# A graph-attention layer on one NeuronCore: edge rows loaded after all of x, layer-norm subtractions on other engines, the first products in two token groups, two weight splits and two output sums later in the order

## The chip, the cores and the metric

The kernel runs on one NeuronCore of a Trainium2 chip. The time is the device time of one execution in microseconds (us); the table gives the median of three runs. A core has five engines that run side by side, each with its own queue of instructions in program order: PE (matrix products), DVE (vector), ACT (scalar activations), POOL (GpSimd) and SP, which here only issues DMA transfers. An instruction that needs a result of another engine, or of a transfer, waits at the head of its queue, and everything behind it in that queue waits with it.

## The reference

N = 384 tokens, 1024 features, 16 heads of 64; a graph of 6528 edges.

```python
h = jnp.maximum(_layernorm(x, axis=-1), 0.0)
q = h @ wq.T + bq;  k = h @ wk.T + bk;  v = h @ wv.T + bv
q2 = (q @ wiq.T + biq).reshape(N, H, D).transpose(1, 0, 2)      # the same for k2, v2
mask = _build_mask(edge_index, edge_type, edge_type_weights, x.dtype)   # -inf where no edge
scores = jnp.einsum('hnd,hmd->hnm', q2, k2) * scale + mask[None]
out = jnp.einsum('hnm,hmd->hnd', softmax(scores), v2)
return x + out.transpose(1, 0, 2).reshape(N, OUT_F) @ wo.T + bo
```

## The kernel before, in words

**Precision.** Every operand of a product is held as two parts in a reduced format, `hi` and `lo` = value - hi. A product of a weight and an activation is three matmuls (`mm3`, L367 to L369): hi by hi, hi by lo, lo by hi.

**Weights.** Seven weight matrices come in 56 chunks of 128 x 1024 (512 KB), numbered w: 0-7 are wv, 8-15 wq, 16-23 wiv, 24-31 wk, 32-47 wiq and wik in turn, 48-55 wo. A chunk goes through `load` (SP issues a DMA into one of three `raw` buffers), `split_hi` (ACT, L77, a cast) and `split_lo` (L82, a subtraction, on DVE or on POOL), into one of four `whl` buffers.

**The head.** SP issues the loads of the three 128-token tiles of x (L96), with the edge rows `er` (L98, 128 x 102 integers) between tile 0 and tile 1, then weight 0, the edge table `ed`, weight 1, biases. PE turns dummy transposes over (`warm`, L309). `key_rows` (L180: three POOL operations L182 to L184 and a store) makes the edge keys row by row in `krow`, from which `key_load` (L205) reads them back into all partitions. For each tile t the layer norm takes mean and variance on DVE (`ln_bn`, `ln_mean`), subtracts the mean in two halves of 512 (`ln_sub`; on ACT by a bias `negm`, on POOL L282, or on DVE L284), transposes on PE (`ln_transpose`, L292) and keeps max(0, .) as hi (ACT, `ln_hi`, L298) and lo (DVE, `ln_lo`, L303). The division by the standard deviation comes later, as a row (`ln_row`). POOL makes both parts of weight 0 (L344, L346) and the low part of weight 1 (L82).

**Projections.** `proj` runs slots: one chunk of 128 outputs by all 384 tokens, 24 matmuls in one PSUM bank. Slot 0 (L411) does its 24 in an order by what is ready: hi-hi for k = 0..7, then lo-hi and hi-lo by halves of k. Meanwhile the edge mask is made: DVE compares keys, POOL scatters values into DRAM.

**The attention loop.** `for i in range(S + LA + 4)` (L767) works step i on 48 pairs of a head and a token tile: score product S(i) (L694, PSUM tag `s`, two banks), mask, minimum and read-out on DVE for i-1 (L700), exponential for i-2 (ACT, L704), normalisation for i-3 (POOL, L709), transposes for i-5 (L714), their split for i-6 (`do_pt`, L723 on ACT, L724 on DVE), products with v (L731). Between them `fill` draws other PE work from generators: first `fill_qk` (the q and k products of chunks 32 to 47), then `fill_o` (the output products `omm`).

At the beginning of a chunk of `fill_qk` a task `qk_head(w)` is queued, which runs at the end of that step (before the loop at once): it loads chunk w+4, splits w+2, and takes one `qk_done` from `pendq`: evacuation of the last bank (L377, L378) and the copies of its halves into `qs` (L557 to L560) or `ks` (L567), DMAs from SBUF to SBUF. `PRE = 84` puts chunks 32, 33, 34 and half of 35 ahead of step 0. With `PAR = 1` odd chunks have their low half on POOL.

In the second half, `wo_prep(k)` splits chunk 48+k at the steps `WSTEPS`; `OPOOL` lists the k with the low half on POOL. After the fourth product of an output bank, `ysum` (L654, DVE) adds the bank to x + bo.

Of the kernel before, what the change touches and what calls it, by code (L numbers as in the profile page):

```python
# [14 lines left out]
N, D, NT, KT, NP = 384, 1024, 3, 8, 8  # L15
# [7 lines left out]
def gnn_kernel(ctx: ExitStack, tc: tile.TileContext, x, edges, erows, etw, wq, wk, wv, wiq, wik, wiv, wo,  # L23
# [6 lines left out]
    nc = tc.nc  # L30
# [9 lines left out]
    NTAB, RNG = 3, EC // 3  # L40
# [3 lines left out]
    def bank(tag):  # L44
        return psum.tile([128, 512], F32, tag=tag, name=tag, bufs={"g": 3, "a": 1}.get(tag, 2))
# [14 lines left out]
    def load(w):  # L60
        if w >= NCH:
            return
        n, m = chunks[w]
        raw[w] = wpool.tile([128, D], F32, tag="raw", name="raw", bufs=3)
        nc.sync.dma_start(raw[w], W[n][m])
# [28 lines left out]
    er = ert[:, :2 * EC].bitcast(I32)  # L94
    for t in range(NT):
        nc.sync.dma_start(xt[t], x[t * 128:(t + 1) * 128, :])  # L96
        if t == 0:
            nc.sync.dma_start(er, erows)  # L98
    load(0)
    ed = const.tile([128, 3 * EC], I32, name="ed")  # L100
    nc.sync.dma_start(ed, edges)
# [78 lines left out]
    def key_rows():  # L180

        nc.gpsimd.tensor_copy(kf, er)  # L182
        nc.gpsimd.tensor_scalar(kf[:, :EC], kf[:, :EC], float(N), None, op0=OP.mult)
        nc.gpsimd.tensor_tensor(krt[:, :EC], kf[:, :EC], kf[:, EC:], OP.add)  # L184
        nc.sync.dma_start(krow.rearrange("c j -> (c j)").rearrange("(p e) -> p e", p=128), krt[:, :EC])
# [10 lines left out]
    def key_load(g, s):  # L196

        if s == 0:
            t = work.tile([128, 2, NT, N], F32R, tag="pt", name="rows")
            krv[g] = t.bitcast(F32).rearrange("p a k n -> p (a k n)")  # L200
        c0, c1 = parts(g)[s]
        dst = krv[g][:, s * PA * 128:(s * PA + c1 - c0) * 128]
        for c in range(c0, c1):
            rows[c] = krv[g][:, (s * PA + c - c0) * 128:(s * PA + c - c0 + 1) * 128]
        nc.sync.dma_start(dst, krow[c0:c1, :].rearrange("c j -> (c j)").partition_broadcast(128))  # L205
# [44 lines left out]
    def ln_bn(t, h):  # L250
        nc.vector.bn_stats(lnt[:, 30 + 12 * t + 6 * h:36 + 12 * t + 6 * h], xt[t][:, h * 512:(h + 1) * 512])

    def ln_mean(t):
        nc.vector.bn_aggr(lnt[:, 2 * t:2 * t + 2],
                          lnt[:, 30 + 12 * t:42 + 12 * t].rearrange("p (a b) -> p a b", a=2))
        if t < 2:
            nc.scalar.mul(negm[:, t:t + 1], lnt[:, 2 * t:2 * t + 1], -1.0)

    def ln_root():
# [17 lines left out]
    def ln_sub(t, c0, c1, eng):  # L277
        src, dst = xt[t][:, c0:c1], xn[t][:, c0:c1]
        if eng is nc.scalar:
            nc.scalar.activation(dst, src, AF.Identity, bias=negm[:, t:t + 1])  # L280
        elif eng is nc.gpsimd:
            nc.gpsimd.tensor_tensor(dst, src, lnt[:, 2 * t:2 * t + 1].to_broadcast([128, c1 - c0]), OP.subtract)  # L282
        else:
            nc.vector.tensor_scalar(dst, src, lnt[:, 2 * t:2 * t + 1], None, op0=OP.subtract)  # L284

    def ln_transpose(t):
        pss = []
        for half in range(2):
            ps = bank("st"[half] if t < 2 else "ga"[half])
            for j in range(4):  # L290
                k = half * 4 + j
                nc.tensor.transpose(ps[:, j * 128:(j + 1) * 128], xn[t][:, k * 128:(k + 1) * 128], ident)  # L292
            pss.append(ps)
        return pss

    def ln_hi(t, half, ps):
        hi = hT[:, 0, half * 4:half * 4 + 4, t * 128:(t + 1) * 128]
        nc.scalar.activation(hi, ps.rearrange("p (k n) -> p k n", k=4), AF.Relu)  # L298
# [7 lines left out]
    def warm(n):  # L306
        for i in range(n):
            ps = bank("g")
            nc.tensor.transpose(ps[:, :128], ident, ident)  # L309

    mask_consts()
    warm(WARM[0])
    key_rows()
    load(2)
    for s in range(NTAB):
        key_load(0, s)
    ln_bn(0, 0)
    ln_bn(0, 1)
    ln_mean(0)
# [6 lines left out]
    ln_bn(1, 0)  # L326
    ln_bn(1, 1)
    ln_mean(1)
    ln_sub(1, 0, 512, nc.scalar)
    ln_sub(1, 512, D, nc.gpsimd)  # L330
    ln_bn(2, 0)
    ln_bn(2, 1)
    ln_mean(2)
    ln_sub(2, 0, 512, nc.vector)
    ln_sub(2, 512, D, nc.vector)
    p1 = ln_transpose(1)
    warm(WARM[2])
    ln_hi(1, 0, p1[0])
    ln_hi(1, 1, p1[1])
    p2 = ln_transpose(2)  # L340
    t0 = wpool.tile([128, 2, D], F32R, tag="whl", name="whl", bufs=4)
    whl[0] = (t0[:, 0, :], t0[:, 1, :])
# [43 lines left out]
    w = 0  # L386
# [18 lines left out]
    def proj(src, dst, bidx, extra=None):  # L405
        nonlocal w
        for m in range(8):
            slot_head(w)
            ps = bank("g")
            if w == 0:  # L410
                for a, b, ks in ((0, 0, range(KT)), (1, 0, range(4)), (0, 1, range(4)), (1, 0, range(4, KT)),  # L411
                                 (0, 1, range(4, KT))):
                    for k in ks:
                        nc.tensor.matmul(ps[:, :N], whl[0][a][:, k * 128:(k + 1) * 128], src[:, b, k, :],  # L414
                                         start=(a == b == k == 0), stop=(b == 1 and k == KT - 1))
            else:
                for k in range(KT):
                    colmm(ps, w, src, k)
                    if w == 1 and k == 3:
                        ln_row()  # L420
                        flush()
            pend.append(lambda ps=ps, m=m: evac_row(ps, dst[:, 0, m, :], dst[:, 1, m, :],
                                                bc[:, bidx * 8 + m:bidx * 8 + m + 1]))
            if extra:
                extra(m)
            w += 1
# [145 lines left out]
    def run_tasks():  # L572
        while tasks:
            tasks.pop(0)()

    def qk_head(w):
        first = w - W0 < 3
        if not first:
            load(w + 4)
            split_hi(w + 2)  # L580
        if pendq:
            pendq.pop(0)()
        if 0 < w - W0 < NTAB:
            mask_select(w - W0)
        if first:
            split_hi(w + 2)
        split_lo(w + 2, nc.gpsimd if (w + 2) % 2 == PAR else None)
        if first:
            load(w + 4)
        if w == W0:  # L590
            mask_select(0)
# [21 lines left out]
    LT, LA = 5, 7  # L613
    PRE, RATE, RATE_O, RATE_E = 84, 7.9, 8, 8
    WSTEPS = (37, 40, 42, 44, 47, 51)
    PAR, OPOOL, ODVE = 1, (2, 3, 6), (2,)

    otile = {}
    oacc = {}
# [31 lines left out]
    def ysum(a, c=(0, 512)):  # L651
        t, h = OT[a]
        y = xb[t][:, h * 512 + c[0]:h * 512 + c[1]]
        nc.vector.tensor_tensor(y, oacc[t, h][:, c[0]:c[1]], y, OP.add)  # L654
        return y

    def fill_o():


        first = [(0, 0), (0, 1), (1, 0), (1, 1), (2, 0), (2, 1)]  # L660
        first += [(a, k) for k in (2, 3) for a in range(3)] + [(a, k) for a in range(3, 6) for k in range(KH)]
        for a, k in first:
            while now[0] < wready[k] or now[0] < 6 * k + OREADY or (k == KH - 1 and now[0] < XSTEP + 3):
                yield 0
            if k == 0:
                oacc[OT[a]] = bank("g")
            omm(*OT[a], k)
            if k == KH - 1:
                ysum(a)
            yield 4  # L670
        bank_step = (0, 0, 0, 49, 50)
        todo = [(a, k) for k in range(KH, 7) for a in range(5)]
        while todo:
            ready = [q for q in todo if now[0] >= max(6 * q[1] + OREADY, wready[q[1]], bank_step[q[0]])]
            if not ready:
                yield 0
                continue
            a, k = ready[0]
            todo.remove(ready[0])
            if k == KH:  # L680
                oacc[OT[a]] = bank("gggss"[a])
            omm(*OT[a], k)
            yield 4
# [83 lines left out]
    for i in range(S + LA + 4):  # L767
        now[0] = i
        r = RATE if len(gens) == 2 else RATE_O if i < S else RATE_E
        fill(r / 2)  # L770
        if i < S:
            do_S(i)
        fill(r / 2)
        if 0 <= i - 1 < S:
            do_ttr(i - 1)
        if 0 <= i - 2 < S:
            do_exp(i - 2)
        if 0 <= i - 3 < S:
            do_norm(i - 3)
        if 0 <= i - LT < S:  # L780
            do_T(i - LT)
        j = i - LA
        if j >= 2 and (j - 2) % 3 == 0 and (j - 2) // 3 < 16:
            do_A((j - 2) // 3)
        if 0 <= i - LT - 1 < S:
            do_pt(i - LT - 1)
        if j >= 3 and (j - 3) % 3 == 0 and (j - 3) // 3 < 16:
            do_ao((j - 3) // 3)
        if j >= 4 and (j - 4) % 6 == 3:
            do_aos((j - 4) // 3)  # L790
        run_tasks()
        if i == XSTEP:
            assert len(gens) < 2
            xb_load()
        if i in WSTEPS:
            wo_prep(wp)
            wready[wp] = i + 2
            wp += 1
# [57 lines left out]
```

## Time and profile before

| | us |
|---|---|
| median of 3 runs | 303.16 (302.75 to 303.68) |
| the profiled execution | 302.19 |
| its span, first to last instruction | 300.5 |
| first product with a weight (L414) starts | 12.26 |
| last matmul ends, modelled | 296.98 |

The granted PE clock is 0.999 of full speed. What PE waited for, by the profile (instruction, releaser: us in total, times, longest):

```profile
PE s L292 <- ACT g L280: 2.0, 2, 1.2
PE g L309 <- POOL ident masks.py:199: 1.4, 1, 1.4
PE s L694 <- DVE s L700: 0.2, 1, 0.2
```

In a timeline a row has the start in us, the length in us, engine, line, operation, output<-input, shapes, the count merged in that row, and in brackets the idle time of the engine before it with what ended it. In the rows of windows each engine has its busy time in the window, and behind them stand the granted PE clock, the busy share of the 16 DMA engines and GB/s. A line number is that of the kernel before.

### The profile page before, as it was taken

To read this page: it belongs to the slowest core of one execution; us is meant where nothing else is said; L and a number is where in the kernel's file an instruction comes from. 1 tells how busy PE (TensorE), PEld (TensorE's weight loads), DVE (VectorE), ACT (ScalarE), POOL (GpSimd) and SP (SyncE) were. 2 spreads that over 40 slices of the span, in tenths; PEclk is the share of its full clock that TensorE was granted. 3 is DMA by queue.
4 is the path that set the end of the run, shared out by engine and by line. 5 is a ranking of instruction groups with operands and counts; after the bars stand their busy time and mean duration, and the time that the engine had idled before them with its cause. 6 is when DMAs were issued, how large, how long until landed. Compare 5 with 4: busy or idle time off the path is not lost.

```text
span 300.5 us, 4961 instructions
## 1 busy us (share of the span) xinstructions
PE 293.1 (98%) x1649; PEld 276.1 (92%) x1649; DVE 200.5 (67%) x492; ACT 154.9 (52%) x289; POOL 155.7 (52%) x164
## 2 busy tenths in 40 slices
PE   7899999999999999999999999999999999999995
PEld 5699999999988889999999999999999998888884
DVE  2959986655956463788865576767576757696523
ACT  3874644333422213554325667777777767676310
POOL 5865766271555785730033737373746467566210
PEclk9999999999999999999999999999999999999999
DMA  7899754642686668475369997646565636910005
GB/s 233 284 297 381 281 164 171 228 143 70 217 238 224 193 217 242 142 274 198 115 169 244 217 221 173 166 127 180 155 170 139 174 81 174 381 41 0 2 0 209
DMA packets 22377, 55.12 MB, mean 183 GB/s; under 512 B 4816, under 2 KB 8400, under 8 KB 22352
## 3 DMA queue, kind: packets, MB, share of 16 engines
q1 hardware_dynamic: 19968, 52.42, 57.7%
q0 software_dynamic: 2064, 1.80, 2.0%
q10 hardware_dynamic: 320, 0.59, 0.8%
q8 instruction: 13, 0.21, 0.3%
q14 instruction: 12, 0.10, 0.1%
HBM read 40.39 MB, written 4.97 MB: 151 GB/s over the span
## 4 chain that ended last, share of the span: by engine, by line
PE 95%; DMA 2%; DVE 1%; ACT 0%; issue 0%; SPq 0%
PE g L369 21%; PE g L367 21%; PE g L368 21%; PE s L694 6%; PE a L731 6%; PE t L714 5%; PE s L369 2%; PE s L368 2%; PE s L367 2%; DMA g<-in_x_dram 2%; PE t L369 2%; PE t L367 2%; PE t L368 2%; PE g L414 1%; PE a L369 1%; PE a L367 1%
## 5 line engine op out<-in xcount | busy, mean ns | idle before, releaser
L367 PE MATMUL g<-g,whl 128*128 128x384 f32 x312 | 106.4, 341 | 0.0
L369 PE MATMUL g<-g,whl 128*128 128x384 f32 x312 | 104.5, 335 | 0.0
L368 PE MATMUL g<-g,whl 128*128 128x384 f32 x312 | 104.2, 334 | 0.0
L228 POOL DMA_INDIRECT tab<-val,idx x51 | 57.6, 1129 | 40.3 <-issue 11.3
L77 ACT ACTIVATE whl<-raw 128x1024 fp32r<-128x1024 f32 x51 | 53.4, 1051 | 31.7 <-PE g L369 20.1
L709 POOL TENSOR_TENSOR e<-e,s 128x384 f32<-128x384 f32 x48 | 39.2, 830 | 41.2 <-DVE s L708 32.9
L368 PEld LDWEIGHTS g<-g,whl 128*128 128x128 f32 x312 | 58.7, 188 | 0.0
L367 PEld LDWEIGHTS g<-g,whl 128*128 128x128 f32 x312 | 58.6, 188 | 0.0
L369 PEld LDWEIGHTS g<-g,whl 128*128 128x128 f32 x312 | 58.5, 188 | 0.0
L82 DVE TENSOR_TENSOR whl<-raw,whl 128x1024 fp32r<-128x1024 f32 x41 | 50.2, 1224 | 9.6 <-ACT whl L77 7.9
L82 POOL TENSOR_TENSOR whl<-raw,whl 128x1024 fp32r<-128x1024 f32 x11 | 26.5, 2412 | 35.6 <-ACT whl L77 31.8
L383 ACT ACTIVATE g<-f,bc 128x384 fp32r<-128x384 f32 x24 | 14.8, 618 | 53.1 <-DVE f L382 46.8
L704 ACT ACTIVATE e<-e,s 128x384 f32<-128x384 f32 x48 | 29.4, 612 | 13.0 <-DVE s L700 13.0
L724 DVE TENSOR_TENSOR pt<-t,pt 128x384 fp32r<-128x384 f32 x48 | 26.4, 550 | 13.9 <-ACT pt L723 13.3
L723 ACT ACTIVATE pt<-t 128x384 fp32r<-128x384 f32 x48 | 23.2, 484 | 13.9 <-PE t L714 13.3
L700 DVE CUSTOM_DVE_ANT_0 e<-s,ma 128x384 f32<-128x384 f32 x48 | 26.3, 550 | 2.0 <-PE s L694 1.8
L694 PE MATMUL s<-ks,qs 128*128 128x384 f32 x96 | 25.3, 344 | 0.3 <-DVE s L700 0.2
L714 PE MATMUL t<-ident,e 128*128 128x128 f32 x144 | 23.5, 271 | 0.0
L382 DVE TENSOR_TENSOR f<-g,rrow 128x384 f32<-128x384 f32 x24 | 13.3, 555 | 13.5 <-PE g L369 7.6
L714 PEld LDWEIGHTS t<-ident,e 128*128 128x128 f32 x144 | 18.8, 140 | 3.1
L378 DVE SCALAR_TENSOR_TENSOR nat<-g,bc,nat 128x384 fp32r<-128x384 f32 x16 | 9.9, 618 | 16.4 <-ACT nat L377 14.4
L731 PE MATMUL a<-pt,vhl 128*128 128x384 f32 x96 | 20.8, 351 | 0.0
(147 smaller groups left out, 414.8 us busy)
## 6 DMA issues: line engine op xcount, KB each, us to landing
ks<-nat SPq DMA_DIRECT2D x30, 192.0 KB
raw<-in_wv_dram SPq DMA_DIRECT2D x8, 512.0 KB
raw<-in_wq_dram SPq DMA_DIRECT2D x8, 512.0 KB
raw<-in_wiv_dram SPq DMA_DIRECT2D x8, 512.0 KB
raw<-in_wk_dram SPq DMA_DIRECT2D x8, 512.0 KB
raw<-in_wiq_dram SPq DMA_DIRECT2D x8, 512.0 KB
raw<-in_wik_dram SPq DMA_DIRECT2D x8, 512.0 KB
raw<-in_wo_dram SPq DMA_DIRECT2D x8, 512.0 KB
```

The source lines that it names most:

```text
L77: nc.scalar.activation(dst[0], raw[w], AF.Copy)
L82: (eng or nc.vector).tensor_tensor(lo, raw[w], hi.bitcast(F32), OP.subtract)
L228: nc.gpsimd.indirect_dma_start(out=tabs[c // RNG], out_offset=bass.IndirectOffsetOnAxis(ap=idx[:, c:c + 1], axis=0), in_=val[:, c:c + 1], ...
L367: nc.tensor.matmul(ps, lhi, rhi, start=first, stop=False)
L368: nc.tensor.matmul(ps, lhi, rlo, start=False, stop=False)
L369: nc.tensor.matmul(ps, llo, rhi, start=False, stop=last)
L694: nc.tensor.matmul(ps[:, :N], qs[:, o, t * 128:(t + 1) * 128], ks[:, o, s, :], start=(s == 0), stop=(s == 1))
L704: nc.scalar.activation(es[i], es[i], AF.Exp, bias=s[:, 0:1], scale=-1.0, accum_out=s[:, 1:2])
L709: nc.gpsimd.tensor_tensor(es[i], es[i], s[:, 2:3].to_broadcast([128, N]), OP.mult)
L714: nc.tensor.transpose(ps[:, k * 128:(k + 1) * 128], es[i][:, k * 128:(k + 1) * 128], ident)
L724: nc.vector.tensor_tensor(lo, pv, hi.bitcast(F32), OP.subtract)
L731: nc.tensor.matmul(ps[:, :N], vhl[:, k, p, 2 * o:2 * o + 2, :], pts[h][:, s, k, :], start=(k == 0 and s == 0), stop=(k == 2 and s == 1))
```

## The change

1. The load of `er` is issued after the three tiles of x.
2. Tile 1's first half is subtracted on DVE in place of ACT, tile 2's second half on ACT in place of DVE; `negm` is made for tiles 0 and 2. In DVE's queue tile 1's subtraction now stands before tile 2's statistics.
3. `key_rows`, `load(2)` and the three `key_load` are emitted after the subtractions of tile 1, and so `key_rows` follows both subtractions in POOL's queue.
4. Tile 1's transposes and hi parts are emitted before tile 2's statistics.
5. Slot 0 does hi-hi for tokens 0 to 255 and then for 256 to 383: 32 matmuls in place of 24.
6. `qk_head` of chunks 35 and 36 only takes its `qk_done` and puts the split of chunks 37 and 38, and the loads of 39 and 40 behind each, off to the ends of steps 2 and 3 (`qk_split`).
7. `ysum` after the fourth product is put in a list, which is emptied after the step's L700 (or when a bank is opened). Two sums of step 43 move behind the L700 of that step; the others keep their place.
8. Chunk 52 (k = 4 of wo) has its low half on POOL.

The order of all other instructions on each engine stays as it was.

```diff
@@ loads
     for t in range(NT):
         nc.sync.dma_start(xt[t], x[t * 128:(t + 1) * 128, :])
-        if t == 0:
-            nc.sync.dma_start(er, erows)
+    nc.sync.dma_start(er, erows)
@@ ln_mean
-        if t < 2:
+        if t != 1:
             nc.scalar.mul(negm[:, t:t + 1], lnt[:, 2 * t:2 * t + 1], -1.0)
@@ head
     mask_consts()
     warm(WARM[0])
-    key_rows()
-    load(2)
-    for s in range(NTAB):
-        key_load(0, s)
     ln_bn(0, 0)
...
     ln_mean(1)
-    ln_sub(1, 0, 512, nc.scalar)
+    ln_sub(1, 0, 512, nc.vector)
     ln_sub(1, 512, D, nc.gpsimd)
+    key_rows()
+    load(2)
+    for s in range(NTAB):
+        key_load(0, s)
+    p1 = ln_transpose(1)
+    warm(WARM[2])
+    ln_hi(1, 0, p1[0])
+    ln_hi(1, 1, p1[1])
     ln_bn(2, 0)
     ln_bn(2, 1)
     ln_mean(2)
     ln_sub(2, 0, 512, nc.vector)
-    ln_sub(2, 512, D, nc.vector)
-    p1 = ln_transpose(1)
-    warm(WARM[2])
-    ln_hi(1, 0, p1[0])
-    ln_hi(1, 1, p1[1])
+    ln_sub(2, 512, D, nc.scalar)
     p2 = ln_transpose(2)
@@ proj, slot 0
-                for a, b, ks in ((0, 0, range(KT)), (1, 0, range(4)), (0, 1, range(4)), (1, 0, range(4, KT)),
-                                 (0, 1, range(4, KT))):
+                al = (0, N)
+                for a, b, ks, (n0, n1) in ((0, 0, range(KT), (0, 256)), (0, 0, range(KT), (256, N)),
+                                           (1, 0, range(4), al), (0, 1, range(4), al), (1, 0, range(4, KT), al),
+                                           (0, 1, range(4, KT), al)):
                     for k in ks:
-                        nc.tensor.matmul(ps[:, :N], whl[0][a][:, k * 128:(k + 1) * 128], src[:, b, k, :],
-                                         start=(a == b == k == 0), stop=(b == 1 and k == KT - 1))
+                        nc.tensor.matmul(ps[:, n0:n1], whl[0][a][:, k * 128:(k + 1) * 128], src[:, b, k, n0:n1],
+                                         start=(a == b == k == n0 == 0), stop=(b == 1 and k == KT - 1))
@@ loop
+    defer = []
+
+    def qk_split(w):
+        split_hi(w)
+        split_lo(w, nc.gpsimd if w % 2 == PAR else None)
+        load(w + 2)
+
     def qk_head(w):
         first = w - W0 < 3
+        if 3 <= w - W0 < 5:
+            pendq.pop(0)()
+            defer.append((now[0] + 6 - w + W0, w + 2))
+            return
         if not first:
             load(w + 4)
             split_hi(w + 2)
...
-    PAR, OPOOL, ODVE = 1, (2, 3, 6), (2,)
+    PAR, OPOOL, ODVE = 1, (2, 3, 4, 6), (2,)
...
+    ysums = []
+
+    def flush_y():
+        while ysums:
+            ysum(ysums.pop(0))
@@ fill_o
             if k == 0:
+                flush_y()
                 oacc[OT[a]] = bank("g")
             omm(*OT[a], k)
             if k == KH - 1:
-                ysum(a)
+                ysums.append(a)
...
             if k == KH:
+                flush_y()
                 oacc[OT[a]] = bank("gggss"[a])
@@ step
         if 0 <= i - 1 < S:
             do_ttr(i - 1)
+        flush_y()
...
         run_tasks()
+        while defer and defer[0][0] <= i:
+            qk_split(defer.pop(0)[1])
```

## The prediction

> **What bounds the kernel now.** I read the page first, then PE's waits, then the timeline of each engine where PE is late. The busy shares:
>
> ```profile
> PE 293.1 (98%) x1649; PEld 276.1 (92%) x1649; DVE 200.5 (67%) x492; ACT 154.9 (52%) x289; POOL 155.7 (52%) x164
> ```
>
> PE ends the chain (95% of it), so a change pays only where PE stands still. A PE busy time has a modelled end and hides small stalls, so I also took PE's starts in the trace: a 384-column matmul starts 173 ns after the one before, a 512-column one 227, a 128-column one 108. Beyond these PE loses 11.4 us in the whole run, in four places. (1) Before the first weight product at 12.26: warm-up and layer norm. (2) At 166.19 (0.15+0.11) and 172.08 (0.24+0.08), both score products L694: 0.57 together. (3) At 262.92 (0.40+0.11) and 265.24 (0.15+0.11), L694 again: 0.76. (4) Some 0.085 at changes of tile, all through the loop, which no edit touches.
>
> Head, POOL and DVE by time (start, length, what, idle before):
>
> ```profile
> 4.35 0.27 POOL L182 CAST er<-er 128x102 f32<-128x102 int32 x1 [1.77 <-DMA er<-in_erows_dram]
> 5.20 0.29 POOL L184 TENSOR_TENSOR kr<-er 128x51 f32<-128x51 f32 x1
> 8.77 1.04 POOL L282 TENSOR_TENSOR g<-g,lnt 128x512 f32<-128x512 f32 x1 [1.96 <-DVE lnt L254]
> 9.81 1.36 POOL L344 CAST whl<-raw 128x512 fp32r<-128x512 f32 x2
> 11.14 2.72 POOL L346 TENSOR_TENSOR whl<-raw,whl 128x512 fp32r<-128x512 f32 x2
> 14.20 2.41 POOL L82 TENSOR_TENSOR whl<-raw,whl 128x1024 fp32r<-128x1024 f32 x1
> ...
> 7.16 1.29 DVE L251 BATCH_NORM_STATS2 lnt<-g 128x6 f32<-128x512 f32 x2 [1.47 <-DMA g<-in_x_dram]
> 10.12 1.34 DVE L284 TENSOR_SCALAR g<-g,lnt 128x512 f32<-128x512 f32 x2
> ```
>
> The reader is to see that POOL has no pause from 8.77 to 16.61, and that the key rows (4.35 to 5.49) lie in a pause in which it waits for tile 1. The last of that chain, weight 1's low half (L82, ends 16.61), is read by PE's L368 at 16.68: no slack. Tile 1 is what the chain waits for: its landing is 7.14.
>
> Loop, the same view:
>
> ```profile
> 164.45 1.21 DVE L82 TENSOR_TENSOR whl<-raw,whl 128x1024 fp32r<-128x1024 f32 x1
> 165.58 0.55 DVE L700 CUSTOM_DVE_ANT_0 e<-s,ma 128x384 f32<-128x384 f32 x1
> 164.56 2.64 SPq L567 DMA_DIRECT2D ks<-nat  x4
> ...
> 259.76 1.23 DVE L82 TENSOR_TENSOR g<-raw,g 128x1024 fp32r<-128x1024 f32 x1 [0.39 <-ACT g L77]
> 260.91 1.49 DVE L654 TENSOR_TENSOR g<-g,g 128x512 f32<-128x512 f32 x2
> 262.31 0.55 DVE L700 CUSTOM_DVE_ANT_0 e<-s,ma 128x384 f32<-128x384 f32 x1
> 262.92 0.62 PE L694 MATMUL s<-ks,qs 128*128 128x384 f32 x2 [0.23 <-DVE s L700]
> ```
>
> Twice a mask-and-maximum (L700) stands behind a weight split in DVE's queue, and the next score product needs its PSUM bank. The stall at 172.08 is another: its `ks` copies, issued at 164.56 and 165.07, land at 171.04 and 171.99, behind weights 39 and 40 (issued 159.97 and 162.88) in a DMA queue that is full:
>
> ```profile
> 164.00:168.00 4.00, 4.00 (x23) 3.70 (x22) 3.33 (x10) 2.30 (x7) 1.23 (x2) 1.00 1.07 225
> 168.00:172.00 4.00, 4.00 (x25) 3.66 (x23) 2.28 (x8) 3.21 (x9) 3.90 (x4) 1.00 1.07 219
> ```
>
> (second last: DMA share, 1.07 of all 16 engines).
>
> **The change part by part.** The sums stand against the profiled execution: 302.19, span 300.5, 1.7 around it. The runs' median, 303.16, lies 0.97 higher; I carry the difference over to it.
>
> *Edge rows behind x.* `er` leaves the place between tiles 0 and 1. Its 128 packets took 25 ns each, 0.2 us on 16 engines: the lower bound of what tile 1 gains. Tile 1's 16 completions come from 5.36 to 7.14, tile 0's only from 3.73 to 4.13: some engines took 0.7 to 1.06 us for tile 1's first packets, those of tile 2, which follows a tile directly, 0.3 to 0.6. If `er` causes the whole spread, tile 1 lands 1.6 earlier, the upper bound. I take 0.2 plus the 0.4 by which tile 2's first packets were better: d = 0.6.
>
> *Key rows behind both POOL subtractions.* L182 to L184, 4.35 to 5.49, cost 1.14 and move from a pause into the chain L282, L344, L346, L150, L82. All of it is delayed by 1.14 and advanced by d. With `er` landing behind tile 2 (8.49 before) and L282 ending near 9.2 there is no wait for it. Weight 1's low half then ends at 16.61 + 1.14 - 0.6 = 17.15, and L368 starts at 17.2 instead of 16.68: **+0.5**. With d = 0.2 it is +0.9. With a large d the first cast cannot start before weight 0 (landed 9.76, less the 0.2 of `er`): -0.2 is the best.
> Queued behind the key rows on SP are their store, load(2), three row loads and load(3): store and load(2) are issued at about 10.8 instead of 5.52 and 7.15. Weight 2 needs 1.3 us of queue (8 packets per engine at 159 ns), so it lands near 13.5, before ACT's 14.02. The rows and weight 3 come about 1 us later; ACT waits for weight 3 at 20.88 already, but PE's slot 3 starts only at 25.2 (16.5 + 48 x 0.173 + 0.4) and its split ended at 23.20: 2.0 of cover for 1 us. Nothing, unless the delay passes 2.
>
> *Subtractions.* Tile 1's first half goes from ACT (mul and L280: 8.72 to 9.68) to DVE; DVE's two took 1.34 beside POOL's casts, whereas a DVE cast of twice the elements with POOL idle (L75, 248.98) took 0.68. So one is about 0.35 alone. Tile 2's second half goes to ACT (about 0.96) and its transposes end near 12.0 - d. The new DVE half starts 0.05 us before POOL's L282. Bounds by rows: no collision, 0; or POOL waits one length, +0.35. I take 0, since in the old place the same collision (2 x 0.35 in POOL's 4.05 of casts) goes away.
>
> [...]
>
> *Tokens 0 to 255 first.* Eight 256-column products (0.120 each, the last L367 of the kernel) and eight of 128 (0.108) replace eight of 0.173: +0.44 of PE work. It lies under the wait for weight 1: with PE starting near 11.5 its 32 products end near 16.1, before 17.15. If that cover goes (d near 1.6), 0.44 would be seen, inside the bounds above.
>
> *Two splits and loads put off* (weights 37, 38; loads 39, 40). L82 of 38 leaves L700's way: 0.26 gained. `ks` stands ahead of both loads, 0.31 gained: copies issued near 163.7, four at 0.94 of queue each, the first pair down by 167. Splits still in time: ACT casts 37 after 163.6, POOL ends its low half near 167.1, PE's slot 37 opens near 168. What is late next is load 39, issued near 166 instead of 159.97; 128 packets behind `ks` (empty near 168.7) land it near 170.3. ACT's cast of 39 waits for it, and behind that stand ACT's exponentials, POOL's split of 39 (2.41) and normalisation 2 (0.83), which PE's transpose 2 needs at 174.7: landing + 1.05 + 2.41 + 0.83 + 0.2 of hand-overs = 174.8. So 0.1 is given back: **-0.45**; from -0.57 (no wait) to +0.2 (landing at 171.0).
>
> *Output sums, weight 4 on POOL.* L82 (1.23) and two sums leave the way of L700; POOL is idle from 259.6 to 263.1 and takes the split in 2.41, its use comes six steps later. L700 runs at 259.4, before S44. The 0.51 at 262.92 goes; at 265.24 the third sum is still ahead of its L700, so 0.25 stays. **-0.5**, from -0.76 to -0.25.
>
> Sum: +0.5 - 0.45 - 0.5 = **-0.45**; 301.7 on the profiled scale, **302.7** on the median's. Bounds: -0.2 - 0.57 - 0.76 = -1.5 and +1.25 + 0.2 - 0.25 = +1.2.
>
> **The rivals.** (a) *Faster*: `er` was what held tile 1 back, and all loop stalls vanish: -1.5, 301.7. For it: the spread of 1.8 against 0.4. Against: tile 2 and weight 0 start slowly too, with no `er` before them. (b) *Slower*: load 39 comes too late. Issue to landing was 6.0 for weight 39 and 7.4 for weight 40 in this queue; with 6.0 after 166 it lands at 172.0 and transpose 2 waits 1.7. Sum +0.5 - 0.57 + 1.7 - 0.5 = +1.1, 304.3. It decides from 170.8 on (slower than before at all). Against: at 166 only `ks` stands before it. (c) *The loop edits do nothing*: the stalls move to the next score products; +0.5 of the head is left, 303.7. Against: DVE is 67% busy, so room to catch up exists.
>
> **How the numbers follow.** Forecast 0.40, with its own range 302.0 to 303.6; (a) 0.30; (b) 0.16; (c) 0.14. 0.3% is 0.9 us, about what a measurement of this kernel can tell from no change (its runs spread over 0.93). Forecast and (c) are mostly within it: same 0.52; (a) and the forecast's fast edge: faster 0.32; (b): slower 0.16. The range goes from (a)'s 301.6 to 304.0, short of (b)'s end.
>
> **What would show it.** Tile 1 landing near 6.5, L184 ending after L282, L82 ending near 17.2, a wait of about 1 us before PE's first L368 (slot 1); no stall at the fourth and seventh score products; ACT idle before its cast of 39; L700 ahead of the L654 pair. The forecast is wrong if L82 of weight 1 ends before 16.5 or after 18, or if PE waits more than 0.5 at transpose 2.

## The result, and the profile after

The changed kernel is slower: 305.58 us median (303.91 to 307.68, 14 runs) against 302.46 (302.13 to 304.32, 14 runs) for the kernel before on the same chip. The ratio of the means is 1.0087, 95% interval 1.0062 to 1.0113; all ratios below are of means. The profiled execution took 306.30, its span 304.6 (before: 302.19 and 300.5).

A line number is that of the kernel whose row is shown: the score product L694 is L714 in the changed kernel, L700 is L720, and the evacuation L377 and L378 (high half on ACT, low half on DVE) is L376 and L377.

First the page of the changed kernel: busy time, and the granted PE clock in 40 slices of 7.6 us. Then what PE waited for (instruction, releaser: us in total, times, longest).

```profile
PE 294.0 (97%) x1657; PEld 278.1 (91%) x1657; DVE 201.4 (66%) x491; ACT 154.9 (51%) x289; POOL 158.8 (52%) x165
...
PEclk9999999999999999999999979999999999999999
```

```profile
PE s L714 <- DVE s L720: 3.2, 1, 3.2
...
PE g L291 <- DVE g L283: 1.4, 1, 1.4
PE s L291 <- ACT g L279: 1.0, 1, 1.0
```

One wait of 3.2 us before a score product (L714, which was L694) is new, and one slice shows less than full clock. The other two waits are in the head, at the layer norm's transposes (L291). The timeline around the new wait, by engine (SP's queue, ACT, DVE, PE):

```profile
163.75 2.40 SPq L568 DMA_DIRECT2D ks<-nat  x4
166.19 0.75 SPq L65 DMA_DIRECT2D raw<-in_wik_dram  x1
...
172.28 1.06 ACT L77 ACTIVATE whl<-raw 128x1024 fp32r<-128x1024 f32 x1 [5.53 <-DMA raw<-in_wik_dram]
173.25 0.56 ACT L376 ACTIVATE nat<-g,bc 128x384 fp32r<-128x384 f32 x1
...
168.11 0.54 DVE L720 CUSTOM_DVE_ANT_0 e<-s,ma 128x384 f32<-128x384 f32 x1
...
173.84 0.62 DVE L377 SCALAR_TENSOR_TENSOR nat<-g,bc,nat 128x384 fp32r<-128x384 f32 x1 [5.11 <-ACT nat L376]
174.38 0.55 DVE L720 CUSTOM_DVE_ANT_0 e<-s,ma 128x384 f32<-128x384 f32 x1
...
171.47 0.33 PE L368 MATMUL g<-g,whl 128*128 128x384 f32 x1
174.99 0.62 PE L714 MATMUL s<-ks,qs 128*128 128x384 f32 x2 [3.18 <-DVE s L720]
```

The kernel before, same load, same cast and the evacuation behind it:

```profile
159.97 0.33 SPq L65 DMA_DIRECT2D raw<-in_wik_dram  x1
...
167.39 1.04 ACT L77 ACTIVATE whl<-raw 128x1024 fp32r<-128x1024 f32 x1
168.34 0.56 ACT L377 ACTIVATE nat<-g,bc 128x384 fp32r<-128x384 f32 x1
```

Read the changed kernel's rows from the bottom. S(6) needs the PSUM bank of S(4), and the mask-and-maximum of S(4) (L720 at 174.38) frees it: PE is idle for 3.18 us before S(6). In DVE's queue that L720 stands behind L377, the low half of chunk 36's evacuation, before which DVE is idle for 5.11. L377 reads what ACT's L376 writes, and L376 stands in ACT's queue behind the cast of weight 39 (L77). The cast waits 5.53 us for the load that edit 6 put off: issued at 166.19 in place of 159.97; before, the cast did not wait. Three engines are held by one transfer, though none of S(4), L376 and L377 has anything to do with weight 39. By PE's starts the wait costs 3.34 + 0.11 (what the first and the second product of S(6) lose beyond the usual spacing).

The windows of the same stretch (PE, PEld, which is PE's weight load, DVE, ACT, POOL busy; then clock, DMA share, GB/s):

```profile
168.00:172.00 4.00, 3.81 (x23) 3.45 (x22) 0.73 (x4) 0.00 (x0) 1.70 (x2) 1.00 0.97 295
172.00:176.00 4.00, 1.01 (x5) 0.99 (x6) 1.70 (x7) 3.16 (x8) 2.58 (x2) 0.98 0.49 157
176.00:180.00 4.00, 4.00 (x17) 3.90 (x16) 2.77 (x7) 3.15 (x8) 2.16 (x3) 0.59 0.64 185
```

ACT does nothing at all from 168 to 172. After the wait the clock record shows 0.5 from 175.83 to 179.25, 3.41 us in which a 384-column product takes 320 ns in place of 173; PE looks busy (4.00) with 17 matmuls in place of some 25. That costs another 1.5 (5.06 us are lost from 172.5 to 180, 3.45 of them in the wait and 0.1 as always). Six of the 14 runs have a mean clock of 0.994, which is what one such stretch would give (an estimate: 1 - 0.5 x 3.41/304); their median is 306.33. The other eight, at 1.000, have 304.87. A stretch right behind the wait is seen in the profiled run alone, and that the wait makes it is not shown. A run's mean clock does not say where a stretch lies, and the kernel before, which has no such wait in its two profiles, has 0.992 to 0.994 in 7 of its 29 runs on the chip of e5 to e8 and in 2 of 23 on that of e9 to e11 (medians 1.3 and 1.0 above its other runs there), in none of 11 on that of e1 to e4.

The head before (PE):

```profile
12.26 4.41 PE L414 MATMUL g<-g,whl 128*128 128x384 f32 x24
16.50 0.33 PE L367 MATMUL g<-g,whl 128*128 128x384 f32 x1
...
16.85 0.33 PE L369 MATMUL g<-g,whl 128*128 128x384 f32 x1
```

In the changed kernel (DVE, POOL, PE):

```profile
7.12 1.37 DVE L283 TENSOR_SCALAR g<-g,lnt 128x512 f32<-128x512 f32 x1
...
7.16 1.04 POOL L281 TENSOR_TENSOR g<-g,lnt 128x512 f32<-128x512 f32 x1 [0.34 <-DVE lnt L253]
14.17 2.40 POOL L82 TENSOR_TENSOR whl<-raw,whl 128x1024 fp32r<-128x1024 f32 x1 [0.63 <-ACT whl L77]
...
11.03 0.63 PE L291 MATMUL g<-ident,g 128*128 128x128 f32 x4 [1.40 <-DVE g L283]
11.85 4.87 PE L415 MATMUL g<-g,whl 128*128 128x256 f32 x32
16.55 0.33 PE L366 MATMUL g<-g,whl 128*128 128x384 f32 x1
```

The first product starts at 11.85 in place of 12.26, slot 1 at 16.55 in place of 16.50, with no wait between. The output part:

```profile
262.50 0.60 PE L714 MATMUL s<-ks,qs 128*128 128x384 f32 x2
...
264.36 2.41 POOL L82 TENSOR_TENSOR g<-raw,g 128x1024 fp32r<-128x1024 f32 x1 [0.19 <-ACT g L77]
...
269.31 0.62 PE L714 MATMUL s<-ks,qs 128*128 128x384 f32 x2
```

Weight 52's low half is on POOL, the stall of 0.51 is gone, the last one (0.16 + 0.11, at 269.31) stays.

The two profiled executions differ by 4.11: slot 1 +0.05, the new wait +3.45, the two small loop stalls -0.57, half clock +1.5, output -0.5. This makes 3.9; 0.2 is not traced. Without the half clock it is +2.4, which is what separates the eight runs at full clock (304.87) from the median before (302.46).

### The profile page after: what moved, and what is told of

Read it like the earlier page. It is cut to its first block, busy times and chain, and to the rows that moved or that the text cites. A ratio compares the mean times of both kernels' runs of the same rounds, so it can differ in the third digit from the quotient of the medians.

```text
span 304.6 us, 4977 instructions
## 1 busy us (share of the span) xinstructions
PE 294.0 (97%) x1657; PEld 278.1 (91%) x1657; DVE 201.4 (66%) x491; ACT 154.9 (51%) x289; POOL 158.8 (52%) x165
## 4 chain that ended last, share of the span: by engine, by line
PE 91%; DVE 3%; DMA 3%; ACT 1%; issue 0%
PE g L368 20%; PE g L366 20%; PE g L367 20%; PE a L751 6%; PE s L714 5%; PE t L734 5%; PE s L367 2%; PE s L368 2%; PE s L366 2%; DMA raw<-in_wik_dram 2%; PE g L415 2%; PE t L368 2%; PE t L367 2%; PE t L366 2%; DVE lnt L250 1%; DMA g<-in_x_dram 1%
## 5 line engine op out<-in xcount | busy, mean ns | idle before, releaser
L368 PE MATMUL g<-g,whl 128*128 128x384 f32 x312 | 105.0, 336 | 0.0
L227 POOL DMA_INDIRECT tab<-val,idx x51 | 56.8, 1114 | 38.7 <-DMA tab<-val,idx 11.0
L77 ACT ACTIVATE whl<-raw 128x1024 fp32r<-128x1024 f32 x51 | 53.5, 1051 | 35.0 <-PE g L368 21.1
L82 DVE TENSOR_TENSOR whl<-raw,whl 128x1024 fp32r<-128x1024 f32 x41 | 51.0, 1244 | 14.3 <-ACT whl L77 14.3
L368 PEld LDWEIGHTS g<-g,whl 128*128 128x128 f32 x312 | 58.8, 189 | 0.0
L729 POOL TENSOR_TENSOR e<-e,s 128x384 f32<-128x384 f32 x48 | 40.2, 852 | 32.9 <-DVE s L728 23.6
L714 PE MATMUL s<-ks,qs 128*128 128x384 f32 x96 | 25.5, 346 | 3.2 <-DVE s L720 3.2
L720 DVE CUSTOM_DVE_ANT_0 e<-s,ma 128x384 f32<-128x384 f32 x48 | 26.3, 548 | 2.7 <-PE s L714 2.6
L381 DVE TENSOR_TENSOR f<-g,rrow 128x384 f32<-128x384 f32 x24 | 13.3, 555 | 13.9 <-PE g L368 13.9
L377 DVE SCALAR_TENSOR_TENSOR nat<-g,bc,nat 128x384 fp32r<-128x384 f32 x16 | 9.9, 616 | 19.0 <-ACT nat L376 17.0
L714 PEld LDWEIGHTS s<-ks,qs 128*128 128x128 f32 x96 | 17.5, 191 | 5.2 <-DVE s L720 4.5
```

What stands on the lines that cost most here:

```text
L77: nc.scalar.activation(dst[0], raw[w], AF.Copy)
L82: (eng or nc.vector).tensor_tensor(lo, raw[w], hi.bitcast(F32), OP.subtract)
L227: nc.gpsimd.indirect_dma_start(out=tabs[c // RNG], out_offset=bass.IndirectOffsetOnAxis(ap=idx[:, c:c + 1], axis=0), in_=val[:, c:c + 1], ...
L368: nc.tensor.matmul(ps, llo, rhi, start=False, stop=last)
L714: nc.tensor.matmul(ps[:, :N], qs[:, o, t * 128:(t + 1) * 128], ks[:, o, s, :], start=(s == 0), stop=(s == 1))
L720: nc.vector.tensor_tensor_reduce(e, st_ps.pop(i)[:, :N], ma[:, t, :], -0.125, 3.0e38, OP.add, OP.min, s[:, 0:1])
```

## The experiments

Diffs are against the kernel named. "Before" is the median of the kernel before on the same chip.

**e1, e2: edit 6 taken out, and edit 6 alone.**

```diff
     def qk_head(w):
         first = w - W0 < 3
-        if 3 <= w - W0 < 5:
-            pendq.pop(0)()
-            defer.append((now[0] + 6 - w + W0, w + 2))
-            return
...
-        while defer and defer[0][0] <= i:
-            qk_split(defer.pop(0)[1])
```

e1 is the changed kernel with this diff; e2 is the kernel before with the same lines added.

> The changed kernel with edit 6 taken back: chunks 35 and 36 load 39 and 40 and split 37 and 38 where the kernel before does. Theory (the put-off load of weight 39 makes the loss): PE's wait of 3.2 us before the seventh score product and the stretch of half clock after it go, the two small stalls of the kernel before (0.26 and 0.32) come back, and what is left is the head (+0.05 by the trace) and the output part (-0.5): 302.46 - 0.45 = 302.0, ratio 0.9985. Rival (head or output edits cost time that the trace hides, or the splits are not the cause): 303.3 or more, ratio above 1.003.

> The kernel before with edit 6 alone. Theory: the whole loss is here: +3.45 of wait before the seventh score product, -0.57 of the two small stalls, and +1.5 where the clock is halved after the wait: 305.3 to 307, ratio 1.010 to 1.015. Rival (the loss comes from the edits of the head, which shift the loop against the DMA queue): below 304, ratio under 1.005, and no wait over 1 us at the seventh score product.

e1: 302.25 (before 302.40), ratio 0.9994 (0.9971 to 1.0016). e2: 307.38, ratio 1.0152 (1.0123 to 1.0182). The loss is there with edit 6 alone and gone without it. e2's profiled execution (305.10) has the wait before the seventh score product, 3.46 + 0.11, but no half clock; three of its four runs have clocks of 0.989 to 0.994 and 307.2 to 308.4. Its window after the wait, to be set beside the one above:

```profile
172.00:176.00 4.00, 1.13 (x7) 1.10 (x8) 1.72 (x8) 3.27 (x8) 2.70 (x2) 1.00 0.42 129
176.00:180.00 4.00, 4.00 (x28) 3.94 (x26) 3.16 (x7) 3.32 (x8) 2.05 (x3) 1.00 0.65 181
```

The same wait, followed from 176 to 180 by 28 matmuls at a clock of 1.00, where the changed kernel did 17 at 0.59: so the halving is a second cost, which did not come in this run. One thing expected of e1 did not come: the two small loop stalls of the kernel before did not return in its profile (see e12).

**e3: the load of 39 alone put back.** Against the changed kernel:

```diff
         if 3 <= w - W0 < 5:
+            if w == W0 + 3:
+                load(w + 4)
             pendq.pop(0)()
...
         split_lo(w, nc.gpsimd if w % 2 == PAR else None)
-        load(w + 2)
+        if w != W0 + 5:
+            load(w + 2)
```

> The changed kernel with one line moved: the load of weight 39 is issued at the head of chunk 35, as before the change; both splits and the load of 40 stay put off. Theory (the landing of load 39 is the cause): it lands near 166 in place of 172.2, ACT's cast of 39 no longer waits for it, the wait before the seventh score product falls from 3.2 to at most 0.35 (its ks copies now stand behind one weight), and no half clock follows: 301.8 to 302.3, ratio 0.998. Rival (the late splits, not the load): the wait stays over 2 us and the time over 305.

301.27 (301.24 to 301.46), ratio 0.9962 (0.9950 to 0.9975). Timeline (SP's queue, ACT, PE):

```profile
159.19 0.33 SPq L65 DMA_DIRECT2D raw<-in_wik_dram  x1
...
166.93 1.05 ACT L77 ACTIVATE whl<-raw 128x1024 fp32r<-128x1024 f32 x1
168.00 0.58 ACT L376 ACTIVATE nat<-g,bc 128x384 fp32r<-128x384 f32 x1
...
171.90 0.51 PE L717 MATMUL s<-ks,qs 128*128 128x384 f32 x2
```

The cast of 39 starts at 166.93 with no wait, the evacuation follows at once, and S(6) runs without one. Both splits and the load of 40 are still late, and the time is below before's: it is the load of 39 that costs.

**e4: the load late, the evacuation ahead of the cast.** Against the changed kernel:

```diff
+        if w == W0 + 5:
+            pendq.pop(0)()
         if not first:
             load(w + 4)
             split_hi(w + 2)
-        if pendq:
+        if pendq and w != W0 + 5:
             pendq.pop(0)()
```

> The changed kernel with one order turned round: chunk 37 takes its qk_done (evacuation of chunk 36 on ACT and DVE, then its copies) before the cast of weight 39 and not after. The load of 39 stays as late as it is, about 172. Theory (the blocked cast held the evacuation, this DVE's queue, and this the fourth mask-and-maximum): the wait before the seventh score product falls from 3.2 to under 0.5; PE then waits at transposes 2 or 3, behind POOL's low half of 39, for 1 to 2.5 us: 302.5 to 304.5. Rival (the late load itself holds the score product by another way, the DMA queue or a buffer): the wait at the seventh score product stays near 3 us, 305.5.

303.01 (302.93 to 303.12), ratio 1.0019 (1.0006 to 1.0032). Timeline (ACT, POOL, PE):

```profile
167.84 0.58 ACT L376 ACTIVATE nat<-g,bc 128x384 fp32r<-128x384 f32 x1 [0.97 <-ACT e L726]
172.19 1.07 ACT L77 ACTIVATE whl<-raw 128x1024 fp32r<-128x1024 f32 x1 [3.77 <-DMA raw<-in_wik_dram]
...
173.34 2.39 POOL L82 TENSOR_TENSOR whl<-raw,whl 128x1024 fp32r<-128x1024 f32 x1 [3.53 <-ACT whl L77]
...
171.74 0.51 PE L716 MATMUL s<-ks,qs 128*128 128x384 f32 x2
...
176.56 0.55 PE L736 MATMUL t<-ident,e 128*128 128x128 f32 x3 [1.54 <-POOL e L731]
```

The load is as late as in the changed kernel (cast at 172.19), yet S(6) runs at 171.74. What is left is a wait at transpose 2 behind POOL's low half of 39: 1.70 by PE's starts. So half of the long wait came from the order on ACT's queue, the other half from the landing itself. PE's pause is 1.54 here, and none of the four runs has a lower clock (all 1.000).

**e5: weight 3 ahead of the row loads.** Against e3:

```diff
     load(2)
-    for s in range(NTAB):
-        key_load(0, s)
...
     load(3)
+    for s in range(NTAB):
+        key_load(0, s)
```

> The kernel with load 39 early (301.27, profiled 301.46) and one more order turned round: weight 3 is loaded ahead of the three row loads in place of behind them. There weight 3 landed at 22.52 and PE waited 0.31 + 0.11 at the first product of slot 3 (24.90), behind ACT's cast, DVE's low half and the evacuation of slot 0 that stands after it in DVE's queue. Theory (the head pays by row loads and weight 3 that come later, 0.76 in the changed kernel and 1.66 here, against a cover of about 1.3): weight 3 lands before 17, the wait at slot 3 goes, 301.0 or less. Rival (rows 1.3 later hold DVE's key comparison instead): the wait stays or grows, 301.3 or more.

301.30 (301.08 to 301.46), ratio 0.9948 (0.9929 to 0.9966), on a chip where before is 302.77. Weight 3 lands at 16.81, and the wait at slot 3 is gone from the profile. The time, 301.0 or less by the theory, is that of e3 (301.27), but e3 ran on another chip, where before is 302.40. The two ratios differ by 0.0014, which is about the 0.42 of the wait, and their intervals overlap. So whether the wait costs time is not shown; it was seen in one profile, of the slowest of e3's four runs.

**e6, e7, e8: head edits alone, output edits alone, edge and key rows alone.** On the kernel before: e6 has edits 1 to 5, e7 has 7 and 8, e8 has only

```diff
-        if t == 0:
-            nc.sync.dma_start(er, erows)
+    nc.sync.dma_start(er, erows)
...
-    key_rows()
-    load(2)
-    for s in range(NTAB):
-        key_load(0, s)
...
     ln_sub(1, 512, D, nc.gpsimd)
+    key_rows()
+    load(2)
+    for s in range(NTAB):
+        key_load(0, s)
```

> The kernel before with edits 1 to 5 alone. Theory by the two traces (first product of slot 1 at 16.55 in place of 16.50, slot 2 at 18.64 in place of 18.58; plus up to 0.4 of wait at slot 3 where weight 3 lands late): +0.05 to +0.5, 302.4 to 302.9. The prediction's own term for the head was +0.5 at slot 1. Rival (the head gained, and the late load hid it): below 302.0.

> The kernel before with edits 7 and 8 alone. Theory: the wait of 0.40 + 0.11 at the score product near 262.9 goes and the one near 265.2 stays: -0.5, 301.9, ratio 0.9983. Rival (DVE's sums, put off, hold a later score product or the last banks): no gain, 302.4 or more.

> The kernel before with edits 1 and 3 alone: edge rows behind x, key rows and their loads behind both POOL subtractions; tile 1's first half stays on ACT, slot 0 as it was. Theory (the edge rows' load between tiles 0 and 1 made tile 1's late and ragged landing): tile 1 lands near 5.4 in place of 7.14, all 16 completions within 0.5, and POOL's subtraction of tile 1 starts near 7.1. Rival (prediction's estimate, 0.6 of gain): it lands near 6.5. Either way the time stays within 0.5 of before, since POOL's chain has the key rows in it: 302.2 to 302.9.

Before is 302.77 on this chip. e6: 302.32, 0.9990 (0.9975 to 1.0006). e7: 302.28, 0.9985 (0.9967 to 1.0003), with the stall of 0.51 gone from its profile. Both intervals hold 1, so neither part alone can be told from no change by the time. e8: 301.63, 0.9952 (0.9931 to 0.9973). In e8 tile 1 lands at 5.69, its 16 completions within 0.53, and slot 1 starts at 16.36. The time of e8 falls outside what was expected: moving the edge rows and key rows together gains about 1.1 by the medians. Its profile shows 0.14 of that at slot 1 and 0.57 in the loop, where both small stalls are gone. Some 0.2 more goes with the clock: without its 7 runs at 0.992 to 0.994 the kernel before has 302.58 here, and no run of e8 is below 0.998. The rest is not traced.

**e9, e10: which of the head edits cost.** e9 is e8 with e3's loop and edits 7 and 8. e10 is e6 without edit 2:

```diff
-    ln_sub(1, 0, 512, nc.vector)
+    ln_sub(1, 0, 512, nc.scalar)
...
-    ln_sub(2, 512, D, nc.scalar)
+    ln_sub(2, 512, D, nc.vector)
```

> The parts that gained, together, on the kernel before: edits 1 and 3 (edge rows and key rows; alone 301.63), edit 6 with weight 39 loaded at its old place, edits 7 and 8. Tile 1's first half on ACT, slot 0 in 24 products. Theory: the head of the edge-row kernel (slot 1 at 16.37), no wait at the fourth and seventh score products, 0.5 less in the output part: 301.1, at most 301.3 (the changed kernel with load 39 early has 301.27 with its slower head). Rival (the three don't add up: what one gains is waited for elsewhere): 301.6 or more.

> The kernel with the head edits 1 to 5 alone, but edit 2 taken back: tile 1's first half is subtracted on ACT again, tile 2's second half on DVE. Slot 1's first product came 11.06 us (mean of six profiles) after tile 1's landing with edits 1 to 5, and 10.68 with 1 and 3 alone. Theory (DVE's subtraction of tile 1 waits for POOL's, 1.37 in place of some 0.35, and all of tile 2 and ACT's cast of weight 1 come later): 10.6 to 10.8 here. Rival (the order of tile 1's transposes or the 32 products of slot 0 cost it): 11.0 or more.

e9: 301.28 (300.86 to 301.62), ratio 0.9940 (0.9919 to 0.9961), before 302.82. It is the best by ratio, but e3's and e5's intervals overlap it. e10: 302.43, 0.9981 (0.9961 to 1.0000), slot 1 11.32 after the landing: the rival, not the theory. The reason is seen by setting PE's rows of e9 beside those of e11 (e1's kernel, same chip). e9:

```profile
11.90 4.40 PE L413 MATMUL g<-g,whl 128*128 128x384 f32 x24 [0.45 <-ACT g L297]
16.14 0.33 PE L366 MATMUL g<-g,whl 128*128 128x384 f32 x1
```

e11:

```profile
11.96 4.87 PE L415 MATMUL g<-g,whl 128*128 128x256 f32 x32
16.67 0.33 PE L366 MATMUL g<-g,whl 128*128 128x384 f32 x1
```

First product to slot 1 is 4.24 with 24 products and 4.71 with 32. In all 14 profiles of this study it is 4.24 to 4.28, or 4.70 to 4.71: PE never waits in slot 0. Edit 5's eight further products stand in the open, +0.46, and the start of the first product is the same within 0.06.

**e11, e12: two kernels once more.**

> The changed kernel without edit 6 once more, beside the two others on one chip. Its first runs spread from 301.11 to 303.8 with a profile (301.26) near the low end. Theory (the splits and loads in their old place leave a score product or slot 3 to the landing of a transfer, which differs from run to run): again a spread of 1 us or more and a median 0.5 to 1.5 above the kernel with load 39 early. Rival (chance of that chip): a spread under 0.6.

> The kernel before once more, for a second profile. Two things differ between the profiles with the edge rows between tiles 0 and 1 (three) and behind x (nine): tile 1 lands at 6.88 to 7.67 against 5.33 to 5.69, and where the splits of 37 and 38 are in their old place, PE waits before the fourth or seventh score product in two of two against none of five. Theory (both hang on the order of the head): tile 1 lands after 6.8, and PE waits 0.2 or more at the fourth or seventh score product. Rival (the second is chance, the landing of weight 37 in a full queue): tile 1 lands after 6.8, but no such wait is seen.

e11: 301.95 (301.31 to 303.24), 0.9973 (0.9951 to 0.9994). A spread of 1.9 again, but neither its profile nor e1's shows a loop stall, and both profiles are of runs near the low end. So the theory's place for the spread isn't shown; it stays open. e12 (302.60, a single run) is the kernel before. Its ACT and PE rows, then ACT's of the first profile of the kernel before, then ACT's of e8:

```profile
163.08 1.06 ACT L77 ACTIVATE whl<-raw 128x1024 fp32r<-128x1024 f32 x1 [3.62 <-DMA raw<-in_wiq_dram]
...
166.92 0.62 PE L694 MATMUL s<-ks,qs 128*128 128x384 f32 x2 [0.26 <-DVE s L700]
```

```profile
162.35 1.06 ACT L77 ACTIVATE whl<-raw 128x1024 fp32r<-128x1024 f32 x1 [2.26 <-DMA raw<-in_wiq_dram]
```

```profile
161.71 1.06 ACT L77 ACTIVATE whl<-raw 128x1024 fp32r<-128x1024 f32 x1 [1.88 <-DMA raw<-in_wiq_dram]
```

Tile 1 lands at 7.62, and PE waits 0.42 + 0.11 at the fourth score product, as the theory said. With the edge rows between tiles 0 and 1 tile 1 lands at 6.88, 7.14, 7.62 and 7.67 (four profiles), with them behind x at 5.33 to 5.69 (ten). With the splits in place there is a small loop stall in three of three profiles with the edge rows between, in none of five with them behind. The rows show the place: the cast of weight 38 (not 37, as e12's rival has it; the rows name `wiq`, the even chunks). It starts at 162.35, 163.08 and 163.59 in the three profiles with a stall (before, e12, e7), and the stall at the fourth score product grows with it: 0.15, 0.42, 0.85, each + 0.11. In the five without it starts at 161.71 to 161.97. Behind the cast stand, as in the long wait, the evacuation on ACT, its low half on DVE, and here also DVE's split of 38 before L700. So the kernel before already had the chain of the long wait, in small. Weight 38 is issued no later in those three (156.68 to 157.67 against 157.37 to 157.57), but takes 4.7 to 6.8 from issue to cast against 4.3 to 4.5, in a queue that is about as full in both (DMA share from 156 to 160 and to 164: 0.92 and 0.95 before, 0.83 and 1.00 in e7, 0.99 and 1.00 in e8). What carries the order of the head to 160 us is not shown.

## Why the prediction was wrong

The forecast was 302.7 (ratio below 1); the change costs 3.1 by the medians, 0.87% by the means.

*The failing step: load 39.* The prediction had it land near 170.3, with only transpose 2 late behind it, 0.1 in all. Both halves failed.
- The landing. 12 of the 16 completions of the load were there by 170.3, so the sum over packets was right for them; the last came at 172.20, and the cast started at 172.28 (172.17 in e2, 172.19 in e4). Rival (b) took issue to landing from a row of the same queue, 6.0, and had 172.0. An earlier landing was argued from "only `ks` stands before it": the four `ks` copies did stand before it, but weights 40 and 41 came right behind (167.13 and 168.21), and the windows show the DMA share at 0.97 from 168 to 172.
- The queue behind the cast. The prediction named exponentials, POOL's split and normalisation 2, and left out the evacuation L376, which `qk_head` of the same chunk emits right behind the cast, ahead of these. Through it DVE's L377 and the two L720 behind that were held, and PE stopped at S(6), 171.65, 3 us before the transpose that the prediction watched. e4 is rival (b) as it was written: with the evacuation out of the way the wait is at transpose 2, and 1.70 where the rival had 1.7.

*The half clock* (+1.5 in the profiled run, and as much between the medians of the six runs at 0.994 and the eight others) had no term at all.

*Two loop stalls, -0.57.* They went, but e1, e6 and e8 show that they go without edit 6 too. So edit 6 is not needed for this gain; what the prediction gave as the cause (DVE's split in front of L700, the loads in front of `ks`) stands there unchanged in these three. For the stall at 166.19 what decides is when weight 38 lands (see e12): the split of 38 is a link of that chain and was named, the cast's wait of 2.26 for the load and the evacuation between were not.

*Edge rows.* d, the earlier landing of tile 1, was 1.74 (7.14 to 5.40), not 0.6: the spread of its completions fell from 1.77 to 0.37, the case that rival (a) stood on, and the first of them came 0.33 earlier. SP issues tile 1's load at 1.25 in place of 1.72, a gain that the prediction's bounds had left out. e8 shows the gain, of edge rows and key rows together.

*Key rows in POOL's chain, +1.14, and "no slack" at L368.* The key rows did go into the chain. But the low half of weight 1 is the weight operand of the third product of a group (L369 before, at 16.85), not of the second; the chain had 0.24 of slack, and PE had no wait there. What sets slot 1 is the first product's start plus slot 0's own length: 12.26 + 4.25 before, 11.85 + 4.71 after. These give the +0.05 that was measured, a tenth of the predicted +0.5: the first product came 0.41 earlier and slot 0 took 0.46 longer, and it is chance that the two nearly cancel.

*Tokens 0 to 255 first, 0.44 at nothing.* The cover named for it, the wait for weight 1, did not exist in the trace. The text's price without cover was 0.44; e9 against e11 shows 0.46.

*Subtractions at nothing.* DVE's half of tile 1 took 1.37 beside POOL's 1.04, against 0.46 each in e9 (0.92 for two). It was DVE that lost time, 0.91, where the prediction's bound had POOL wait 0.35, and tile 2's statistics behind it started at 8.40 with the tile there at 7.56. The first product started within 0.06 of e9's in e11, so PE's bill for it looks small; that edit 2 was harmless for the time is not shown.

*Weight 3, "2.0 of cover".* In e3 it came 1.66 later than before (22.52) and PE already waited 0.42. Behind the split in DVE's queue stands the evacuation L381 (0.55), whose bank slot 3 needs; the cover is some 1.3, an estimate from 1.66 less the first product's 0.31. It is the same omission as for load 39. In the changed kernel weight 3 came 0.76 later, and PE did not wait.

*Output sums and weight 4, -0.5.* Right in place and size: 0.51 gone, 0.26 left, by the trace; e7's median agrees, though its interval touches 1.

The sum that the traces leave, at full clock: +0.05 + 3.45 - 0.57 - 0.5 = +2.4, and +1.5 more where the clock is halved.

## What to carry to other kernels

When a load is put off, follow the queue of the engine whose instruction waits for it, instruction by instruction, and then the queue of each engine that waits for one of those: here an evacuation right behind a cast that waited 5.53 us on ACT held DVE's queue for 5.11, and through it, for 3.18, the PSUM bank that PE's score product needed. Take a transfer's landing from issue to the last completion of a load in the same queue (6.0 before, 6.01 here), not from bytes alone. Before an edit is costed at nothing under a wait, look in PE's own rows whether that wait exists.

## What was not expected of the hardware

- In the profiled run PE was idle for 3.18 us (3.52 from start to start) and then, from 175.83 on, ran at half clock for 3.41 us. In e2's profile PE was idle for 3.29 us before the same score product, and the clock stayed at 1.00 in the windows behind it. What decides between the two is not shown.
- The edge rows' load, 51 KB in rows of 408 bytes, between two of 512 KB: the tile behind it has its 16 completions 1.5 to 2.3 apart (four profiles: before, where it is 1.77, e2, e7 and e12) in place of 0.4 to 0.5 (the ten others; 0.37 in the changed kernel's).
- Of two instructions that start within 0.05 us of each other (DVE's L283 at 7.12, POOL's L281 at 7.16), the one recorded first was the one that took longer, in all seven profiles with edit 2 (1.37 each, against 0.46 in e9). POOL's took 1.04, as it did in e9 and before.
